# Columns of several groups as 64 columns twice in a tile, any set of groups, first fit in two passes

## The chip, the core and the metric

The kernel runs on one core of a Trainium2 chip. The metric is the device time of one execution in microseconds, the median of three timed runs: 1469.44 us (1468.46 to 1476.89). The profile is of one further execution of the same program.

## The reference

For x of shape (8, 4096, 256), a sparse non-negative adj of (4096, 4096) and a weight W of (256, 256), all float32:

```
A_norm = relu((adj + adj.T) * 0.5)
d      = rowsum(A_norm) ** -0.5           # 0 where the sum is 0
L_norm = I - d[:, None] * A_norm * d[None, :]
out    = layernorm(x + relu(L_norm @ (x @ W)))   # L_norm is shared by the 8 batches
```

Entry (n, m) of adj is drawn with a probability that falls with n and with m, so low rows and columns are dense and the others sparse. The 8 batches of 256 features are treated as 2048 columns, so that the sum is a 4096 x 4096 sparse matrix times a 4096 x 2048 dense one.

## The kernel before, in words

**First stage** (to about 587 us of the profiled execution). Blocks of adj are loaded on SP's queue, transposed on PE (L516), added to their mirror image on DVE (L520), halved and cut at zero on ACT (L524), and stored to `a_dram`. DVE sums each row over groups of 32 columns (L527), and POOL turns the sums into flags, `uses` (L528). The row factors r come from the same sums. g = r * (x W) is formed on PE (L616, L627) and stored to `g_dram`, 4096 rows of 2048 floats (8 KB). Block 0 of the output is multiplied here from whole blocks (L585).

**Second stage.** The other 31 blocks of 128 output rows are worked in 16 units `u` of two blocks (the last has one), in the order `SEQ`. a_dram is symmetric, so the columns that a block needs are rows of a_dram: for a unit, a column m counts only if one of its 8 groups of 32 output rows uses it (4 groups in each block b). The used columns are gathered into tiles of 128: an a-row (32, 128 or 256 floats) and a g-row (2048 floats) for each. The first 2 x 128 columns are used by everybody; they are two resident hub tiles (`g_hub`, a-rows `gh` loaded at L1020).

A tile has two halves of 64 slots, and each half belongs to one kind, a mask of the groups for which its columns are multiplied. There are 15 kinds, `KINDS`: one group alone, pairs of groups, the whole of one block, and 0 for anything (the rest). `CAPS[u][k]` says how many halves the kind k has in unit u and `FIRST[u][k]` where they begin. A tile whose halves have one group each is called alone. In the tables of this case there are 256 tiles, 152 of them alone.

*Lists.* Which column goes into which slot is found on the chip, some units ahead. `patterns` makes the mask of each column on DVE and compares it with the kinds; `count` multiplies by a triangle of ones on PE (L300, L301) to rank the columns of a kind; `place` fits them to the kinds' room, those left over to others, and `count_rest`/`place_rest` the rest; `spread` (L429) and `collect` (L450) turn the slots into lists by products with one-hot tiles, and `index` writes the row numbers `gi` and `ai`. The constants that these steps use are set by memsets on POOL (L218, L219, L225). A dense pass behind the second stage runs only if a list has no room.

*Gathers.* For each tile POOL issues two indirect transfers, the a-rows (L1032) and the g-rows (L1047), into a ring of 12 tiles. A gather is issued once a slot of the ring is free; `gather_ahead` ties it to a product on PE so that the gathers keep pace with the steps.

*Steps.* `steps_of` writes the order of the products. A product takes a piece of PE's array: rows x columns, where 128 rows means all slots of a tile, 64 rows one half of it, and the columns are those of 1, 2 or 4 groups. A step runs over the four chunks c of 512 g-columns, and in each over the products that together fill the array: one of 128x128, two of 128x64, four of 128x32, two of 64x128 or eight of 64x32. The planner picks one such shape for each step. There are 234 steps; 62 belong to the hub tiles. All products of a block add into four banks of PSUM, one for each chunk.

*Blocks end.* When a block's last product is done, ACT evicts its four banks (L788) and DVE adds x and normalises. A unit's block 0 ends four steps ahead of its block 1; in these four steps the lists' products borrow its banks.

The loop over steps is at the end of the function, `product` at L1257 issues one product (L1263).

## Time and profile before

| what | value |
|---|---|
| timed runs, median (lowest, highest) | 1469.44 us (1468.46, 1476.89) |
| profiled execution, its span | 1496.2 us |
| granted TensorE clock, mean | 0.981 |
| first stage, second stage, behind the last product | 0 to 587, to 1484, to 1496 us |
| busy: PE, DVE, POOL, ACT | 1420.1, 1025.2, 745.6, 368.7 us |
| products of the second stage (L1263), busy | 644.8 us (gathered tiles), 226.6 us (hubs) |
| gathers on POOL, a-rows and g-rows | 256 and 256 |
| moved in all; in queue 0, which the gathers use | 540.52 MB; 281.94 MB |

The profiled execution took 26.8 us longer than the median of the timed runs. In the rows that follow, L12 is line 12 of the kernel, PE is TensorE's matmuls and PEld its weight loads. "64*32" is the piece of the array (rows times columns), "64x512" what is moved through it. A float32 product of 512 columns has two matmul records. A matmul's end is modelled and overlaps its successor, so that 600 ns of one isn't the distance between two: that is read from the starts. What stands behind "idle before" is the time for which the engine stood still ahead of the group, and what ended it; "issue" is a wait that the profile doesn't explain.

### The profile page before, as it was taken

Reading aid. Unit: us, or ns where it says so; the run is one execution under the profiler, and the core shown is the slowest. Engines: PE = TensorE matmul, PEld = TensorE weight load, DVE = VectorE, ACT = ScalarE, POOL = GpSimd, SP = SyncE. Lnnn points to the kernel's source line nnn. Section 1 sums busy time; section 2 is a strip of 40 time slices with the busy share of each in tenths; the row PEclk is TensorE's granted clock in tenths of the full one; section 3 lists DMA queues with packets and bytes.
Section 4 is the critical chain, followed back from the end, with each engine's and each line's share of the span. In section 5 each row is a group of like instructions: output and inputs, shape, how many; then the busy total and the mean of one; then the engine's idle time right before and its main releaser. Section 6 shows DMA issues by size and latency. Waiting matters only on the chain.

```text
span 1496.2 us, 20479 instructions
## 1 busy us (share of the span) xinstructions
PE 1420.1 (95%) x6768; PEld 757.9 (51%) x6768; DVE 1025.2 (69%) x3010; ACT 368.7 (25%) x462; POOL 745.6 (50%) x1547
## 2 busy tenths in 40 slices
PE   7998988979999999999999999999999999998996
PEld 6777877766777764333333334333333333333342
DVE  4767558889596752356569678789898079797454
ACT  4555545434544460010100100100110011001102
POOL 2444010010322336756577677577677646666762
PEclk9999999989999999999999999999999999999998
DMA  9999999999999999979899899999999979988995
GB/s 340 360 377 381 406 346 337 393 385 338 379 356 341 371 392 373 373 270 379 332 377 379 338 402 407 366 388 403 398 382 377 387 259 341 354 316 321 402 404 220
DMA packets 215265, 540.52 MB, mean 361 GB/s; under 512 B 17751, under 2 KB 107527, under 8 KB 180839
## 3 DMA queue, kind: packets, MB, share of 16 engines
q0 software_dynamic: 53808, 281.94, 48.5%
q1 hardware_dynamic: 93200, 126.62, 24.4%
q10 hardware_dynamic: 68144, 130.58, 23.0%
q8 instruction: 56, 0.92, 0.2%
q14 instruction: 57, 0.46, 0.1%
HBM read 425.72 MB, written 136.34 MB: 376 GB/s over the span
## 4 chain that ended last, share of the span: by engine, by line
PE 62%; DMA 14%; DVE 11%; issue 7%; POOL 3%; ACT 3%; ACTq 0%; another core or an unknown queue 0%; DVEq 0%; POOLq 0%; SPq 0%
PE py L1263 45%; PE pg L627 8%; DMA a_dram<-sym 6%; DVE sym L520 4%; DMA g<-g_dram,gi 3%; PE xtr L616 3%; PE lead L585 3%; PE tr L516 3%; DMA xin<-in_x_dram 2%; POOL ga L1032 2%; ACT sym L524 1%; DVE sums L527 1%; POOL g L1047 1%; DMA g_dram<-held 1%; PE lists L450 1%
## 5 line engine op out<-in xcount | busy, mean ns | idle before, releaser
L1263 PE MATMUL py<-g,ga 128*32 128x512 f32 (+4 forms) x2880 | 644.8, 606 | 12.3 <-DMA g<-g_dram,gi 7.2
L1263 PEld LDWEIGHTS py<-g,ga 128*32 128x32 f32 (+4 forms) x2880 | 226.0, 138 | 402.0 <-issue 374.4
L1032 POOL DMA_INDIRECT ga<-a_dram,ai x256 | 277.6, 1084 | 181.3 <-issue 62.2
L1047 POOL DMA_INDIRECT g<-g_dram,gi x256 | 284.5, 1111 | 92.9 <-issue 77.6
L788 ACT ACTIVATE y<-py,minus_r 128x512 f32<-128x512 f32 x120 | 80.2, 686 | 796.3 <-PE py L1263 545.9
L627 PE MATMUL pg<-w_sb,xt 128*128 128x256 f32 x1024 | 233.4, 387 | 6.5 <-ACT xt L617 5.7
L1263 PE MATMUL py<-g_hub,gh 128*128 128x512 f32 x496 | 226.6, 601 | 0.5 <-DVE low L465 0.3
L627 PEld LDWEIGHTS pg<-w_sb,xt 128*128 128x128 f32 x1024 | 196.9, 195 | 34.5 <-ACT xt L617 6.6
L520 DVE TENSOR_TENSOR sym<-tr,adj 128x512 f32<-128x512 f32 x256 | 162.3, 684 | 59.0 <-PE tr L516 54.1
L527 DVE TENSOR_REDUCE sums<-sym 128x64 f32<-128x2048 f32 x64 | 145.7, 2282 | 69.5 <-ACT sym L524 69.5
L528 POOL TENSOR_SCALAR uses<-sums 128x64 uint8<-128x64 f32 x64 | 26.7, 417 | 271.1 <-DVE sums L527 236.9
L516 PE MATMUL tr<-ident,adj 128*128 128x128 f32 x1024 | 137.1, 281 | 20.5 <-DVE sym L520 14.3
L1263 PEld LDWEIGHTS py<-g_hub,gh 128*128 128x128 f32 x496 | 90.5, 190 | 123.6 <-issue 116.8
L524 ACT ACTIVATE sym<-sym 128x2048 f32<-128x2048 f32 x64 | 122.7, 1917 | 122.8 <-DVE sym L520 118.6
L516 PEld LDWEIGHTS tr<-ident,adj 128*128 128x128 f32 x1024 | 115.8, 143 | 50.9 <-DVE sym L520 31.1
L242 DVE TENSOR_TENSOR_SCAN incl_r<-carry,lists 128x32 f32<-128x32 bf16 x13 | 2.9, 221 | 182.0 <-PE lists L397 176.0
L429 DVE TENSOR_TENSOR hot<-iota_q,at 128x1024 bf16<-128x1024 f32 x64 | 74.5, 1220 | 34.0 <-PE lead L585 32.1
L798 DVE TENSOR_TENSOR xr<-xr,y 128x2048 f32<-128x2048 f32 x31 | 70.8, 2284 | 38.8 <-ACT y L788 32.1
L616 PE MATMUL xtr<-ident,xin 128*128 128x128 f32 x512 | 74.5, 299 | 17.9 <-DVE sym L520 9.0
L831 DVE TENSOR_SCALAR xr<-xr,mv,root 128x256 f32<-128x256 f32 x248 | 85.1, 416 | 1.1
L807 DVE BATCH_NORM_STATS2 stats<-xr 128x6 f32<-128x256 f32 x248 | 84.0, 413 | 1.1
L585 PE MATMUL lead<-gt,strip 128*128 128x512 f32 x176 | 82.4, 593 | 0.0
(164 smaller groups left out, 1040.1 us busy)
## 6 DMA issues: line engine op xcount, KB each, us to landing
adj<-in_adj_dram SPq DMA_DIRECT2D x64, 1024.0 KB
a_dram<-sym ACTq DMA_DIRECT2D x64, 1024.0 KB
out_dram<-xr SPq DMA_DIRECT2D x31, 1024.0 KB
xr<-in_x_dram ACTq DMA_DIRECT2D x28, 1024.0 KB
xin<-in_x_dram SPq DMA_DIRECT2D x44, 512.0 KB
g_dram<-gt ACTq DMA_DIRECT2D x22, 1024.0 KB
xin<-in_x_dram POOLq DMA_DIRECT2D x20, 512.0 KB
g_dram<-held ACTq DMA_DIRECT2D x10, 1024.0 KB
```

Source lines behind the costliest of these rows:

```text
L516: ins = nc.tensor.transpose(pt[:, c * P : (c + 1) * P], tji[:, c, a * P : (a + 1) * P], ident)
L520: nc.vector.tensor_add(sym[:, a, :], pt, tij[:, a, :])
L524: nc.scalar.activation(sym, sym, AF.Relu, scale=0.5)
L527: nc.vector.tensor_reduce(sums, sym.rearrange("p a (c q) -> p a c q", q=E), AX.X, ALU.add)
L585: nc.tensor.matmul(lead[c], lhsT=strip, rhs=g[:, c * S : (c + 1) * S], start=not done, stop=len(done) == NB - 1, skip_group_check=True,)
L616: nc.tensor.transpose(pt[:, k, c, :], xin[b // H][:, b % H + k, c * P : (c + 1) * P], ident)
L627: ins = nc.tensor.matmul(pg[:, k * FO : (k + 1) * FO], lhsT=xt[:, b + k, c, :], rhs=w_sb[:, c, :], start=(c == 0), stop=(c == FC - 1),)
L807: nc.vector.bn_stats(stats[:, b, :], z[:, b, :])
L831: nc.vector.tensor_scalar(z[:, b, :], z[:, b, :], mv[:, b, 0:1], rstd[:, b : b + 1], ALU.subtract, ALU.mult,)
L1032: rows = nc.gpsimd.indirect_dma_start(out=at if both else at[:, : E if one else P], out_offset=None, in_=a_pairs if both else a_groups if ...
L1047: nc.gpsimd.indirect_dma_start(out=gt, out_offset=None, in_=g_dram, in_offset=bass.IndirectOffsetOnAxis(ap=gi[:, t : t + 1], axis=0), boun ...
L1263: return nc.tensor.matmul(py[2 * u + 1 + b][c][cols, :], lhsT=at[ps, off + cols.start : off + cols.stop], rhs=gt[ps, c * S : (c + 1) * S], ...
```

## The change

**Tiles.** A table `UNITS` replaces `KINDS`, `CAPS` and `FIRST`. For each unit it gives the number of alone tiles of each of the 8 groups, a list of kinds (mask, halves, place), the halves of the rest, the order in which the planner meets the tiles, and its two settings, how many tiles it looks at (`reach`) and how far block 1 stands back (`lag`). A mask may be any set of groups. A column goes to the first kind that covers its groups, in two passes: alone tiles and the first 7 kinds, then all kinds; what has no place then is the rest.

An alone tile is as before: 128 columns, one group, 128x32 products. Every other tile is a pair of halves, and a half is now 64 columns that stand twice in the tile: partitions 0 to 63 hold the first 1024 floats of their g-rows and partitions 64 to 127 the other 1024. So a half fills 128 partitions x 1024 floats, and the two halves of a tile lie side by side. A group's product with a half is four products of 64x32, in two rows of the array at once: the upper one writes chunks 0 and 1, the lower one chunks 2 and 3. There are 253 tiles, 133 of them alone, and 120 pairs with 232 halves.

**Gathers.** A pair tile has one gather of a-rows (into one of 8 buffers `gw`, mostly 256 floats wide) and one of g half rows for each half. Of POOL's issues in the second stage:

Before, a run of tiles at the start of the stage; `ga` are a-rows, `g` g-rows, the numbers only tell buffers apart:

```order
L1032 DMA ga_5775<-a_dram,ai_4117 128x32
L1047 DMA g_5739<-g_dram,gi_4115 128x2048
L1032 DMA ga_5776<-a_dram,ai_4117 128x128
L1047 DMA g_5743<-g_dram,gi_4115 128x2048
L1032 DMA ga_5777<-a_dram,ai_4117 128x256
L1047 DMA g_5747<-g_dram,gi_4115 128x2048
```

and after, at the same place:

```order
L1084 DMA ga_5071<-a_dram,ai_3431 128x32
L1102 DMA g_5032<-g_dram,gi_3428 128x2048
L1084 DMA gw_5081<-a_dram,ai_3431 128x256
L1102 DMA g_5036<-g_dram,gi_3428 128x1024 x2
L1084 DMA gw_5082<-a_dram,ai_3431 128x256
L1102 DMA g_5040<-g_dram,gi_3428 128x1024 x2
```

An alone tile keeps its two gathers; a pair tile has three. In the whole stage 512 gathers became 618 (253 of a-rows, 133 of whole g-rows, 232 of half rows). The columns gathered are 29 952 before and after.

**Swaps.** Each half's a-rows are needed in both rows of the array. ACT copies them to the other 64 partitions, into one of 6 buffers `gs`, up to three steps ahead of the tile's first use (`swap_ahead`). On ACT's queue, at the start of the second stage, behind the evictions of block 0 (L912):

```order
L912 ACTIVATE y_5177<-lead_168,minus_r 128x512
L1135 COPY gs_5089<-gw_5081 64x256 x2
L1135 COPY gs_5090<-gw_5082 64x256 x2
L1135 COPY gs_5091<-gw_5083 64x256 x2
L1135 COPY gs_5092<-gw_5084 64x256 x2
```

There are 232 such copies, where ACT's queue had none.

**Steps.** `steps_of` now fills, for each of the 4 columns of 32, the four chunks of a step: with one 128x32 product of an alone tile (four chunks), or with two (half, group) products (two chunks each, in both rows). It takes whatever comes first in its order, so that a step may hold both shapes. On PE, unit 1, the first step of gathered tiles, behind a hub's last product; before:

```order
L1263 MATMUL py_0_3_5872<-g_hub_5719,gh_0_5784 128x512
L1263 MATMUL py_0_0_5869<-g_5727,ga_5772 32x512
L1263 MATMUL py_0_0_5869<-g_5731,ga_5773 32x512
L1263 MATMUL py_0_0_5869<-g_5735,ga_5774 32x512
L1263 MATMUL py_0_0_5869<-g_5739,ga_5775 32x512
L1263 MATMUL py_0_1_5870<-g_5727,ga_5772 32x512
```

and after (products with `gw` or `gs` are of 64x32, those with `ga` of 128x32; `py_0_2` is block 0, chunk 2):

```order
L1365 MATMUL py_0_0_5193<-g_5024,ga_5069 32x512
L1365 MATMUL py_0_0_5193<-g_5028,ga_5070 32x512
L1365 MATMUL py_0_0_5193<-g_5032,ga_5071 32x512
L1365 MATMUL py_0_0_5193<-g_5036,gw_5081 32x512
L1365 MATMUL py_0_2_5195<-g_5036,gs_5089 32x512
L1365 MATMUL py_0_1_5194<-g_5024,ga_5069 32x512
L1365 MATMUL py_0_1_5194<-g_5028,ga_5070 32x512
L1365 MATMUL py_0_1_5194<-g_5032,ga_5071 32x512
L1365 MATMUL py_0_1_5194<-g_5036,gw_5081 32x512
L1365 MATMUL py_0_3_5196<-g_5036,gs_5089 32x512
```

Four alone tiles filled a step; now three do with a half beside them. There are 204 steps: 62 of hubs, 142 others, of which 78 hold both shapes. The first block's end still lies four steps ahead of the unit's end.

**Lists and constants.** The constants come from one table loaded on ACT's queue in place of 752 memsets on POOL. `match` finds the first fitting kind with bit operations on DVE; `count`, `count_more` and `count_rest` rank on PE. A one-hot tile of `collect` is 64 wide instead of 128, and each of its products is issued twice, for the two halves of PE's columns.

The core of the diff:

```
-            with queue("pool"):
-                nc.gpsimd.indirect_dma_start(
-                    out=gt,
-                    out_offset=None,
-                    in_=g_dram,
-                    in_offset=bass.IndirectOffsetOnAxis(ap=gi[:, t : t + 1], axis=0),
...
+            for h in range(1 if who == ALONE else len(pair(u, t))):
+                k = t if who == ALONE else 2 * t + h
+                end = N if who == ALONE else 2 * N + 1
+                with queue("pool"):
+                    nc.gpsimd.indirect_dma_start(
+                        out=gt if who == ALONE else gt[:, h * HG : (h + 1) * HG],
+                        out_offset=None,
+                        in_=g_dram if who == ALONE else g_halves,
+                        in_offset=bass.IndirectOffsetOnAxis(ap=gi[:, k : k + 1], axis=0),
...
+        def swap_ahead(q):
...
+            while swaps and first_use[swaps[0]] <= q + SOON and free(swap_of, swapped % SWAP):
...
+                for h in range(len(pair(u, t))):
+                    to, of = slice((1 - h) * L, (2 - h) * L), slice(h * L, (h + 1) * L)
+                    with queue("act"):
+                        nc.scalar.copy(sw[to, :width], at[of, :width])
...
+                u, t = order[asked]
+                if t >= alone[u] and not free(wide_of, widened % WIDE):
+                    break
                 gather(asked, behind)
```

```
+        while any(todo.values()):
+            near = [t for t in todo if todo[t]][:reach]
+            ops = sorted((op for t in near for op in todo[t]), key=lambda op: turn[op[0]] + lag * op[2])
+            step = []
+            for j in range(QU):
+                at = 0
+                while at < NC:
+                    op = next((op for op in ops if op[3] == j and (op[1] is not None or at == 0)), None)
+                    if op is None:
+                        break
+                    ops.remove(op)
+                    todo[op[0]].remove(op)
+                    step.append((op, at))
+                    at += NC if op[1] is None else NC // 2
+            out.append(step)
...
+                for r in range(2):
+                    ps = slice(r * L, (r + 1) * L)
+                    of = at if r == h else sw
+                    rhs = gt[ps, h * HG + sub * S : h * HG + (sub + 1) * S]
+                    parts.append((2 * r + sub, of[ps, own_rows], rhs))
...
-            for c in range(NC):
-                for op in step:
-                    rows = slice(0, P) if op[1] is None else slice(op[1] * L, (op[1] + 1) * L)
-                    cols = slice(op[3] * E, (op[3] + op[4]) * E)
-                    ins = product(u, op, c, rows, cols, first, op in last)
...
+            for sub in range(NC):
+                for op, at in step:
+                    if at <= sub < at + (NC if op[1] is None else NC // 2):
+                        ins = product(u, op, sub - at, opens[op], last[op])
```

```
     def collect(u, pl):
...
+            for h in range(2):
+                nc.tensor.matmul(
+                    pl[h * L : (h + 1) * L],
+                    lhsT=hot[:, m],
...
+    table = nc.inline_tensor(np.concatenate(parts)[None], name="table").ap()
+    tables = const.tile([P, ends[-1]], I32, name="tables")
+    nc.scalar.dma_start(tables, table.to_broadcast([P, ends[-1]]))
```

919 lines of the change are left out of this document (510 added, 409 removed), and 32 rows, old and new, of tables (CAPS, FIRST).

## The prediction

> **What bounds the kernel now.** The page first, for the balance over the span (busy time and share of each engine, then tenths in 40 slices):
>
> ```profile
> PE 1420.1 (95%) x6768; PEld 757.9 (51%) x6768; DVE 1025.2 (69%) x3010; ACT 368.7 (25%) x462; POOL 745.6 (50%) x1547
> PE   7998988979999999999999999999999999998996
> DMA  9999999999999999979899899999999979988995
> ```
>
> TensorE and the DMA engines are both busy throughout. The windows tell which one is waited for in the second stage (length; busy time of PE, PEld, DVE, ACT, POOL; granted clock; DMA share; GB/s), and the group of its products shows their idle time:
>
> ```profile
> 587.00:1480.00 893.00, 874.26 (x3843) 333.06 (x3841) 617.88 (x2216) 81.06 (x122) 586.70 (x561) 0.99 0.95 362
> 1000.00:1100.00 100.00, 98.25 (x443) 37.88 (x436) 84.04 (x306) 10.88 (x16) 69.92 (x67) 1.00 1.02 401
> L1263 PE MATMUL py<-g,ga 128*32 128x512 f32 (+4 forms) x2880 | 644.8, 606 | 12.3 <-DMA g<-g_dram,gi 7.2
> ```
>
> PE is busy for 874 of 893 us and its products waited 12.3 us in all. So PE's own sequence sets the end; the transfers keep up with little to spare. What the products cost is read from two timelines, of PE and of its weight loads (start, duration, shape of the array's piece, number of records, idle time before):
>
> ```profile
> 587.10 3.60 PE L1263 MATMUL py<-g_hub,gh 128*128 128x512 f32 x8
> 590.63 3.64 PE L1263 MATMUL py<-g,ga 128*32 128x512 f32 x32
> 594.20 3.27 PE L1263 MATMUL py<-g_hub,gh 128*128 128x512 f32 x7
> ...
> 640.47 0.18 PEld L1263 LDWEIGHTS py<-g,ga 64*32 64x32 f32 x16 [0.76 <-DMA g<-g_dram,gi]
> ...
> 645.41 0.20 PEld L1263 LDWEIGHTS py<-g,ga 64*32 64x32 f32 x6 [0.59 <-issue]
> 646.44 0.16 PEld L1263 LDWEIGHTS py<-g,ga 128*32 128x32 f32 x8 [0.84 <-issue]
> 646.90 0.13 PEld L1263 LDWEIGHTS py<-g,ga 128*32 128x32 f32 x4 [0.30 <-issue]
> 647.33 0.13 PEld L1263 LDWEIGHTS py<-g,ga 128*32 128x32 f32 x4 [0.30 <-issue]
> ```
>
> A 512-column product has two records. Steady loads come 0.43 us apart (646.90 to 647.33), so one pass of the filled array over 512 columns takes 0.86 us (0.858 by finer rows), whether it is one 128x128, four 128x32 or eight 64x32. A step is four passes, 3.43 us; from start to start it is 3.53 to 3.57 where the shape changes. So a change costs about 0.09 us when the array is full on both sides. The row at 646.44 matters most: the first load of the new shape stands 0.84 us idle, where within a shape 0.30 is usual. The next shape's weights aren't loaded while the old one streams. Every change of the second stage looks like this; no row shows products of two shapes at once, because the old order has one shape in a step.
>
> **The change, part by part.** *Products.* The old order has 234 steps, 936 passes and 156 changes: 936 x 0.858 + 156 x 0.093 = 817.6 us. With stalls in the 64x32 steps (27.9, below), list products and waits this fills the 893 us. The new order has 204 steps, of which 62 are hubs and 78 mix 128x32 with 64x32 inside each chunk. Two readings bound it.
>
> If the two shapes share the array, each column of 32 goes at its own pace and only changes to and from 128x128 count: 792 passes and 31 changes, 682.4 us, 135 less than before.
>
> If a change waits for the old shape to end, as at 646.44, the mixed chunk falls apart. In the order shown above, three 128x32 products fill three quarters of a pass; then two 64x32 products take a pass for a quarter of the array; then three 128x32 again. This step makes 8 passes and 8 changes, 7.6 us instead of 3.43. Going through the whole order so gives 1180 passes and 717 changes: 1180 x 0.858 + 717 x 0.093 = 1079.1 us, 261.5 more than before.
>
> I take the second. Of the rows there are, 646.44 is the nearest: the same two shapes in succession. It is not proof, since all pieces of the array were occupied there; but the weights could have been loaded ahead of it, as they are within a shape, and weren't.
>
> The Trainium skill, TensorEngine Tiling (Array Packing), section Key Properties, says "Mode switching requires drain: Changing tiling mode (not just tile) drains the TensorE", and its list of configurations keeps 128x32 and 64x32 apart. The trace agrees as far as it goes (0.84 us of idle loads at each change); by this rule the sum is the second one, and without it the first.
>
> *Lists.* The products that collect the lists double from 512 to 1024, each for 64 columns instead of 128.
>
> ```profile
> 723.04 0.32 PEld L450 LDWEIGHTS <-hot 128*128 128x128 bf16 x10 [0.62 <-issue]
> L225 POOL MEMSET group_of<- 64x1 bf16 x304 | 29.1, 96 | 10.9
> L524 ACT ACTIVATE sym<-sym 128x2048 f32<-128x2048 f32 x64 | 122.7, 1917 | 122.8 <-DVE sym L520 118.6 <-DMA g_dram<-gt 4.2
> L788 ACT ACTIVATE y<-py,minus_r 128x512 f32<-128x512 f32 x120 | 80.2, 686 | 796.3 <-PE py L1263 545.9 <-remote 117.8 <-DVE root L826 34.7
> L617 ACT COPY xt<-xtr 128x512 f32<-128x512 f32 x128 | 67.9, 593 | 52.7 <-PE xtr L616 51.7 <-ACT held L652 0.4
> ```
>
> At 0.032 us each (10 in 0.32) 512 more cost 16 us, or nothing if two halves run side by side; I take 10.
>
> *Constants.* 752 memsets leave POOL's program for one table (the largest group, 29.1 us, is shown). They lay in the first stage, where POOL is a quarter busy: nothing gained.
>
> *Swaps.* ACT gets 232 copies of 64x256 or 64x128. The nearest row, a 128x512 copy, takes 593 ns; an upper bound is 232 x 0.593 = 138 us, a lower one half of it. ACT is busy 81 of 893 us in this stage, and a swap is asked for three steps ahead, over 10 us: nothing, hidden by ACT's idle time. Evictions of L788 queue behind a swap whose a-rows are late, and the next unit's products wait for those evictions. At most one step (3.5 us) at one tile in ten, some 40 us; below nothing I see no way.
>
> *Gathers.* Each of the 120 pair tiles brings its g in two half rows: 618 gathers for 512, over nearly the same bytes.
>
> ```profile
> 568.10 1.06 POOL L1032 DMA_INDIRECT ga<-a_dram,ai  x1 [0.82 <-DMA a_dram<-diag]
> ...
> 911.83 0.95 POOL L1032 DMA_INDIRECT ga<-a_dram,ai  x1 [0.30 <-issue]
> 913.09 1.01 POOL L1047 DMA_INDIRECT g<-g_dram,gi  x1 [0.30 <-DMA g<-g_dram,gi]
> 914.41 0.94 POOL L1032 DMA_INDIRECT ga<-a_dram,ai  x1 [0.30 <-issue]
> ...
> 1461.58 1.00 POOL L1047 DMA_INDIRECT g<-g_dram,gi  x1 [0.99 <-DMA g<-g_dram,gi]
> ...
> L1047 POOL DMA_INDIRECT g<-g_dram,gi x256 | 284.5, 1111 | 92.9 <-issue 77.6 <-DMA g<-g_dram,gi 10.1 <-DMA gh<-a_dram 2.3
> L1032 POOL DMA_INDIRECT ga<-a_dram,ai x256 | 277.6, 1084 | 181.3 <-issue 62.2 <-PE py L1263 51.3 <-PE lists L300 20.0
> L1020 POOL DMA_DIRECT2D gh<-a_dram x62 | 36.2, 584 | 25.1 <-PE py L1263 10.6 <-DMA g<-g_dram,gi 6.0 <-issue 3.2
> ```
>
> From start to start an a-gather takes 1.26 us and a g-gather 1.32 (rows at 911.83 to 914.41); with the groups' means (1084 and 1111 ns) and the same 0.30 between, 1.39 and 1.42. A half-row gather has as many rows, so I price it like a whole one; half of that is its lower bound. With 62 hub loads at 0.9: 253 x 1.26 + 365 x 1.32 + 56 = 856 us, at most 253 x 1.39 + 365 x 1.42 + 56 = 926. While PE takes 1079 us this is hidden. If PE takes only 682, it is the bound.
>
> **The sum.** 1496.2 + 261.5 + 10 = 1767.7 us for a profiled execution. The span stands 26.8 us above the median of the timed runs, 1469.4; taking the difference over, **1741 us**. Its own range: without lists, 1725, and some overlap at the ends of runs, down to 1690; with 40 us of swap waits, 1780; so 1690 to 1800.
>
> **The rivals.** *Shapes share the array, POOL sets the pace.* For it: pieces in different columns touch nothing in common, and no row of before shows them refusing. Against it: 646.44. Then the last gather starts at 568 + 856 to 926 = 1424 to 1494 instead of 1461.6; the 34.6 us behind it stay, less the 26.8: 1432 to 1502, middle about 1465, no change.
>
> *Shapes share it and the gathers keep up: faster.* One mechanism, at POOL: a half-row gather costs well under a whole one. It decides from a POOL sum below about 845 us (568 + 845 + 34.6 - 26.8 = 1421). At half the price, 232 gathers save 153 us, POOL needs 703 and the transfers bind: 893 us x 362 GB/s = 323 MB, at the best window's 401 GB/s 806 us. From 587, with 13 us behind the last product, less 26.8: about 1380. Between the two, 1420.
>
> *The stalls of the 64x32 steps are real.* The seven 64x32 steps of before take longer than their 3.55 us. The first (640.47 to 646.44) takes 5.97; the last is
>
> ```profile
> 1342.26 0.15 PEld L1263 LDWEIGHTS py<-g,ga 64*32 64x32 f32 x8 [0.76 <-DMA g<-g_dram,gi]
> ...
> 1354.12 0.30 PEld L1263 LDWEIGHTS py<-g,ga 128*128 128x128 f32 x2 [0.89 <-issue]
> L1263 PE MATMUL py<-g,ga 64*32 64x512 f32 x384 | 44.9, 660 | 8.3 <-issue 4.0 <-DMA g<-g_dram,gi 3.6
> L1263 PE MATMUL py<-g,ga 64*128 64x512 f32 x112 | 25.9, 602 | 0.0
> ```
>
> 11.86 us. Together the seven take 52.7, where 7 x 3.55 is 24.9: 27.9 too much, with nothing named as the cause. This is nearly what the span has over the median (26.8), so I hold it for something of the profiled execution alone. If the timed runs have it too, 384 records cost 27.9 us, and the 6416 of the change up to 466 more: 1900 and above.
>
> The Trainium skill (the same page, section Restrictions and Gotchas) says that different row tiles cannot access one PSUM bank at the same time. Before, both halves of a chunk write one bank; now they write two. By this rule the stalls would go with the change, and the time stay with the other cases; but the 64x128 products write one bank from two halves as well, and stand at 602 ns without a stall.
>
> **How the numbers follow.** Shapes wait for each other: 0.50 (1741). Shared and POOL-bound: 0.25 (1465). Shared and faster: 0.18 (1420). Stalls or swap waits beyond that: 0.07 (1900). The likeliest is 1741. Since the shared cases hold 0.43, the range takes in most of them: 1425 to 1800; left out are the stalls and the fastest part of the shared cases, together near 0.15. About 1% (1455 to 1484) is what a measurement can tell from no change. Faster: all but a little of 0.18, and a quarter of the POOL case, 0.24. Same: nearly half of the POOL case and a little more, 0.13. Slower: the rest, 0.63.
>
> **What would show it.** Right: in a mixed step the weight loads of 64x32 start 0.7 us or more after those of 128x32, each chunk takes about 1.9 us, POOL waits for PE more than now, and DMA falls to about 280 GB/s in the second stage (323 MB over some 1155 us). Wrong: mixed steps of 3.4 to 3.6 us, PE idle before L1365 by gathers, POOL busy for over 75 us in each 100 (0.95 of 1.26 us, since the 0.30 between gathers isn't counted). If the stalls belong to the profiled execution, its span will stand further above the timed median than now.

## The result, and the profile after

The changed kernel takes 1979.99 us (median of four runs, 1974.80 to 1987.03) against 1469.54 us for the kernel before: a ratio of 1.3465 [1.3422, 1.3508], 510 us slower. The forecast was 1741 us, with a range to 1800: the direction is right, the size is 239 us short. The profiled execution has a span of 1980.0 us and is one of the four timed runs.

The page of the changed kernel, to be held against the three lines of the page before (busy times; granted clock and DMA share in 40 slices):

```profile
PE 1768.7 (89%) x11912; PEld 717.0 (36%) x11912; DVE 1047.9 (53%) x2771; ACT 456.4 (23%) x694; POOL 810.7 (41%) x887
PEclk9999998999999999899899998879997898999998
DMA  9999998899998684477894856487892483898296
```

The DMA engines, 0.95 busy in the second stage before, now have holes. The clock dips in the same part of the span. The second stage as one window (columns as in the prediction's windows), and the groups of its products:

```profile
598.40:1966.80 1368.40, 1223.92 (x8943) 296.70 (x8943) 613.86 (x2006) 171.42 (x357) 695.06 (x668) 0.94 0.69 242
```

```profile
L1365 PE MATMUL py<-g,gw 64*32 64x512 f32 x3208 | 596.4, 618 | 28.7 <-DMA g<-g_dram,gi 28.7
L1365 PE MATMUL py<-g,gs 64*32 64x512 f32 x3208 | 596.2, 618 | 9.1 <-DMA g<-g_dram,gi 8.9
L1365 PE MATMUL py<-g,ga 128*32 128x512 f32 x1064 | 420.3, 637 | 92.8 <-DMA g<-g_dram,gi 92.7
```

The stage is 1368 us long where it was 896 (587.1 to 1483.2). PE is busy for 1224 of them, 347 more than before, and idle for 145, where it was idle for 19. So there are two losses: PE has more to do, and it waits for g. The waits of PE over the whole execution (us, times, longest):

```profile
PE py L1365 <- DMA g<-g_dram,gi: 130.3, 44, 7.3
...
PE q L416 <- DVE ahead_of L369: 13.2, 1, 13.2
PE py L1365 <- DVE low L582: 11.5, 6, 3.1
```

130 us of waiting for gathers stand where the kernel before had 7.2.

**More to do.** The weight loads of a mixed step, two chunks of it:

```profile
1305.09 0.14 PEld L1365 LDWEIGHTS py<-g,ga 128*32 128x32 f32 x4 [0.84 <-issue]
1306.07 0.10 PEld L1365 LDWEIGHTS py<-g,gs 64*32 64x32 f32 x1 [0.84 <-issue]
...
1307.07 0.14 PEld L1365 LDWEIGHTS py<-g,ga 128*32 128x32 f32 x2 [0.84 <-issue]
1308.04 0.10 PEld L1365 LDWEIGHTS py<-g,gw 64*32 64x32 f32 x1 [0.84 <-issue]
```

The shapes take turns. The idle time of 0.84 us that stood at one step in several before now stands twice in every chunk, and a chunk takes 1.98 us (1305.09 to 1307.07) where a filled pass takes 0.86. This is the forecast's second reading, row for row.

**Waiting, and its second price.** One step with a late tile, on PE:

```profile
1282.35 1.04 PE L1365 MATMUL py<-g,ga 128*32 128x512 f32 x2
1284.20 0.61 PE L1365 MATMUL py<-g,gw 64*32 64x512 f32 x1 [0.80 <-DMA g<-g_dram,gi]
...
1289.81 1.03 PE L1365 MATMUL py<-g,gw 64*32 64x512 f32 x1 [4.56 <-DMA g<-g_dram,gi]
...
1298.52 1.92 PE L1365 MATMUL py<-g,ga 128*32 128x512 f32 x4 [6.79 <-DMA g<-g_dram,gi]
1300.36 1.06 PE L1365 MATMUL py<-g,gw 64*32 64x512 f32 x1
...
1304.08 0.64 PE L1365 MATMUL py<-g,gs 64*32 64x512 f32 x1
```

PE waits 4.56 us and then 6.79 us. Behind each wait the records take 1.03 to 1.06 us instead of 0.61, until about 1304. As windows (the last three columns are granted clock, DMA share and GB/s):

```profile
1298.50:1304.00 5.50, 5.49 (x16) 0.59 (x16) 0.00 (x0) 1.21 (x3) 4.28 (x5) 0.50 0.90 318
1304.00:1310.00 6.00, 6.00 (x64) 1.41 (x70) 0.00 (x0) 0.81 (x2) 3.55 (x5) 0.99 1.04 386
```

PE runs at half its clock (0.50) for some microseconds after it has stood still. The Trainium skill (TensorE: Matmul & The Clock Gate, Part 1) says that the array falls to half its clock after at least one idle window of about 3.4 us, and comes back after at least one busy window of that length; these rows agree, with 5.6 us of half speed behind the second wait. So a wait of this length is paid twice. A short one isn't: behind the 0.80 us at 1284.20 the record still takes 0.61 us.

POOL isn't short of time when this happens. Its timeline ahead of the late step, and its groups:

```profile
1265.24 0.96 POOL L1084 DMA_INDIRECT gw<-a_dram,ai  x1 [19.87 <-issue]
1266.51 0.99 POOL L1102 DMA_INDIRECT g<-g_dram,gi  x1 [0.30 <-DVE slot L523]
1267.80 1.04 POOL L1102 DMA_INDIRECT g<-g_dram,gi  x1 [0.30 <-issue]
```

```profile
L1102 POOL DMA_INDIRECT g<-g_dram,gi x365 | 394.4, 1081 | 118.8 <-issue 106.0 <-DMA g<-g_dram,gi 7.7 <-DMA gh<-a_dram 1.4
L1084 POOL DMA_INDIRECT ga<-a_dram,ai x133 | 141.0, 1060 | 295.6 <-PE py L1365 242.3 <-issue 24.8 <-PE lists L508 23.2
L1084 POOL DMA_INDIRECT gw<-a_dram,ai x120 | 133.8, 1115 | 251.4 <-issue 205.2 <-ACT y L912 24.1 <-PE py L1365 15.3
```

POOL stood idle for 19.87 us, then issued gathers back to back, and this burst came too late. Over the stage it waits 258 us for PE (242.3 and 15.3; 51.3 before). The planner looks at up to nine tiles at once, so many of the ring's 12 tiles are half used and none is free; then several come free together, and the pacing asks for only one or two of them in a step. Counted through the order in the code, the unit that ends here has all 12 places taken and ten of them half used four steps before its end, and all 12 free one step before it.

**The sum.** I added up, over the second stage, the distance from each product's start to the next one's, and put each to what stood between the two (records of over 0.9 us count as half clock; a distance at a wait holds the record ahead of it as well, about 0.43 us):

| us | before | after |
|---|---|---|
| products, shape unchanged | 750.4 | 701.8 |
| a change of shape between (before 130, after 625 times) | 68.1 | 326.5 |
| at half clock, shape unchanged; changed | 7.0; 1.0 | 69.8; 40.9 |
| waits for g | 10.2 | 160.1 |
| lists' products between | 34.6 | 49.3 |
| waits for DVE (lists) | 9.7 | 20.0 |
| waits without a name | 15.2 | 0 |
| second stage | 896 | 1368 |

About half of what the half-clock rows hold would be there at full clock too. So the products, with their changes, went from 822 to some 1084 us (1139 less 55); late gathers cost 150 in waits, and the clock some 50, which I put to them as well; lists and list waits cost 25, the stage begins 11 us later, and the 15 us of waits without a name are gone. Together this is the 484 us between the two profiled spans.

### The profile page after: what moved, and what is told of

The parts are those of the page before. It is cut to its first block, busy times and chain, and to the rows that moved or that the text cites. A ratio compares the mean times of both kernels' runs of the same rounds, so it can differ in the third digit from the quotient of the medians.

```text
span 1980.0 us, 30359 instructions
## 1 busy us (share of the span) xinstructions
PE 1768.7 (89%) x11912; PEld 717.0 (36%) x11912; DVE 1047.9 (53%) x2771; ACT 456.4 (23%) x694; POOL 810.7 (41%) x887
## 3 DMA queue, kind: packets, MB, share of 16 engines
q0 software_dynamic: 69840, 287.63, 40.9%
## 5 line engine op out<-in xcount | busy, mean ns | idle before, releaser
L1365 PE MATMUL py<-g,gw 64*32 64x512 f32 x3208 | 596.4, 618 | 28.7 <-DMA g<-g_dram,gi 28.7
L1365 PE MATMUL py<-g,gs 64*32 64x512 f32 x3208 | 596.2, 618 | 9.1 <-DMA g<-g_dram,gi 8.9
L1365 PE MATMUL py<-g,ga 128*32 128x512 f32 x1064 | 420.3, 637 | 92.8 <-DMA g<-g_dram,gi 92.7
L1102 POOL DMA_INDIRECT g<-g_dram,gi x365 | 394.4, 1081 | 118.8 <-issue 106.0
L1084 POOL DMA_INDIRECT ga<-a_dram,ai x133 | 141.0, 1060 | 295.6 <-PE py L1365 242.3
L1135 ACT COPY gs<-gw 64x256 f32<-64x256 f32 (+1 forms) x232 | 90.5, 391 | 648.0 <-DMA gw<-a_dram,ai 637.5
L1084 POOL DMA_INDIRECT gw<-a_dram,ai x120 | 133.8, 1115 | 251.4 <-issue 205.2
L1365 PE MATMUL py<-g_hub,gh 128*128 128x512 f32 x496 | 224.5, 610 | 11.5 <-DVE low L582 11.5
L1365 PEld LDWEIGHTS py<-g,ga 128*32 128x32 f32 x1064 | 56.8, 110 | 421.9 <-issue 402.1
L1365 PEld LDWEIGHTS py<-g,gw 64*32 64x32 f32 x3208 | 116.7, 108 | 251.8 <-issue 238.3
L912 ACT ACTIVATE y<-py,minus_r 128x512 f32<-128x512 f32 x120 | 78.7, 687 | 527.7 <-PE py L1365 515.3
L1365 PEld LDWEIGHTS py<-g,gs 64*32 64x32 f32 x3208 | 116.7, 108 | 224.7 <-issue 219.0
```

Of the source, the lines that this page charges most:

```text
L912: nc.scalar.activation(y.rearrange("p b o -> p (b o)")[:, c * S : (c + 1) * S], py[c], AF.Relu, scale=minus_r[:, i : i + 1],)
L1084: rows = nc.gpsimd.indirect_dma_start(out=at[:, :width], out_offset=None, in_={2: a_pairs, ALONE: a_groups}.get(who, a_rows), in_offset=ba ...
L1102: nc.gpsimd.indirect_dma_start(out=gt if who == ALONE else gt[:, h * HG : (h + 1) * HG], out_offset=None, in_=g_dram if who == ALONE else ...
L1135: nc.scalar.copy(sw[to, :width], at[of, :width])
L1365: ins = nc.tensor.matmul(banks[c][cols, :], lhsT=rows, rhs=rhs, start=first, stop=last, skip_group_check=True,)
```

## The experiments

The kernel before took 1469 to 1471 us on some of the chips used and 1488 to 1497 us on others. Every ratio is with its runs on the same chip. Each chip was used in one sitting only, so that whether the chip or the sitting makes the difference isn't known; "chip" stands for both here. The changed kernel itself ran only where the kernel before takes 1469 us, while e1 to e8 ran on chips of the slower kind: a time of theirs set against 1979.99 us holds the chip's difference as well, which was not measured for the changed kernel.

**First group: the shapes, or the gathers?** *e1: no change of shape.* Each half product as two 128x32 ones instead of four 64x32: the same array area, one shape. A product then sums over both partition halves, which is not the reference's sum.

```
-                for r in range(2):
-                    ps = slice(r * L, (r + 1) * L)
-                    of = at if r == h else sw
-                    rhs = gt[ps, h * HG + sub * S : h * HG + (sub + 1) * S]
-                    parts.append((2 * r + sub, of[ps, own_rows], rhs))
+                of = at if sub == 0 else sw
+                rhs = gt[:, h * HG + sub * S : h * HG + (sub + 1) * S]
+                parts.append((2 * h + sub, of[:, own_rows], rhs))
```

> Each (half, group) is multiplied by two 128x32 products in its column of the array instead of four 64x32, so that all gathered products have one shape; gathers, swaps, lists, steps and their order stay. (The two halves of a tile are mixed up in this: that part of the product is changed.) Theory, a change of shape lets the old shape run out: 792 passes and about 90 changes, 690 us of PE instead of about 1100; the gathers then set the pace, 1430 to 1600 us. Rival, the late gathers alone make the change slow: they are the same, so 1900 to 2000 us. Rival, 64x32 products are slow by themselves: also below 1600, told apart by the kernel with steps of one shape.

Measured: 1783.83 us, ratio 1.1946 [1.1864, 1.2027]. PE's waits of this kernel:

```profile
PE py L1363 <- DMA g<-g_dram,gi: 223.0, 83, 8.1
```

The changes' distances fell from 367 us to 8.9, and the time by some 196 us (on a chip where the kernel before is 23 us slower), so the drain is real. The time lies above the theory's 1430 to 1600 us and below the rival's 1900: with the products faster, the waits for g rose from 130 to 223 us and the mean clock fell to 0.913. The drains had been covering part of the gathers' lateness: there are two losses, and neither is the whole.

*e2: the shapes sorted within a step.* First all 128x32 products of a step, then all 64x32: 141 changes for 667.

```
+            for part in (True, False):
...
-                    if at <= sub < at + (NC if op[1] is None else NC // 2):
+                        if (op[1] is None) == part and at <= sub < at + (NC if op[1] is None else NC // 2):
```

> Within each step all 128x32 products come first, over the four chunks, then all 64x32; nothing else moves. Changes fall from 717 to 182, passes from 1180 to 1098: 1098 x 0.858 + 182 x 0.12 = 964 us of PE for 1098. Theory, changes let the array run out: 135 us less, about 1845 us. Rival, late gathers: within 20 us of 1980. Rival, 64x32 products slow by themselves: within 20 us of 1980.

Measured: 1918.27 us, ratio 1.2846 [1.2758, 1.2934]. This is 62 us less than the changed kernel, where 135 were expected. The distances at changes hold 74 us instead of 367 (each has a pass's 0.43 us in it), but the products in between rose from 702 to 903: each shape's share of a step still fills only part of the columns, and an empty column takes the same 0.86 us. The dear thing about a mixed step is less the change than the broken passes.

*e3: one shape in a step.* The planner fills a step with one shape, from five tiles at most; 227 steps.

```
-            near = [t for t in todo if todo[t]][:reach]
+            near = [t for t in todo if todo[t]][: min(reach, 5)]
...
+            for single in (True, False):
+                left, step = [op for op in ops if (op[1] is None) == single], []
...
+            out.append(best[1])
```

> The planner gives each step one shape, four 128x32 or up to eight 64x32 in each chunk, and looks at 5 tiles at most; tiles, gathers and swaps stay. 227 steps, 886 passes, 110 changes: 773 us of PE for 1098. Theory, changes let the array run out: 325 us less, and what then is left of the waits (250 us with the slow clock behind them) is open: 1480 to 1680 us. Rival, 64x32 products slow by themselves: there are as many as before, 1900 us or more. Rival, late gathers: 1900 us or more.

Measured: 1746.49 us, ratio 1.1669 [1.1592, 1.1746], above what was expected. The products cost what they should (754 us, and 44 at changes, where before has 750 and 69), and still 58 us of waits for g, 99 us at half clock and 87 us of waits without a name remain.

*e4: gathers as soon as there is room.* The pacing of the gathers is dropped.

```
-            for _ in range(room if behind is None else min(room, 1 + (room > SLACK))):
+            for _ in range(room):
```

> Gathers are issued for every free place of the ring at each step, instead of one, or two when over five places are free. Order of the products as in the change. Theory, shapes 258 us and late gathers with the slow clock behind them 250 us of the loss: if the pace of one or two tiles a step makes them late, 1750 to 1900 us; if the ring itself is full, within 20 us of 1980. Rival, late gathers alone: below 1700 us.

Measured: 2024.19 us, ratio 1.3555 [1.3461, 1.365]. None of the expected ranges holds this time. PE's idle time for g fell from 130 to 20 us with the reach of nine left as it was, so the pacing has its share in the lateness. But waits without a name rose to 113 us, and PE stood idle 11 us for evictions and 21 for a source that the profile calls "remote". On this chip issuing earlier is no cure; what it does on a chip without the unnamed waits was not run.

*e6: five tiles in view.* Only the planner's reach changes; 652 shape changes stay.

```
-            near = [t for t in todo if todo[t]][:reach]
+            near = [t for t in todo if todo[t]][: min(reach, 5)]
```

> The change, with shapes mixed as in it, but its planner looks at 5 tiles at most instead of 5 to 9. Passes 1155 for 1180, changes 652 for 717: 29 us less of PE. A tile is now asked for two steps or more ahead of its first product (30 tiles of the change only one or two), so the ring holds fewer tiles half used. Theory B, tiles held in the ring: the waits for gathers (160 us) and the slow clock behind them (about 55 us lost) fall by over half, 1820 to 1870 us. Theory A, the third gather: as many gathers as before, so 1940 us or more.

Measured: 1869.63 us, ratio 1.2564 [1.2514, 1.2615]. PE's waits for g and the second stage as a window:

```profile
PE py L1365 <- DMA g<-g_dram,gi: 9.0, 2, 5.3
```

```profile
597.80:1855.90 1258.10, 1189.21 (x8945) 323.67 (x8943) 611.63 (x2006) 170.61 (x357) 692.98 (x668) 0.97 0.77 263
```

130 us of waits became 9, with the same gathers and the same POOL time. So POOL's total isn't what made them late. With e4 this says that a tile is late when it is asked for too few steps ahead, which the reach and the pacing settle together: counted through the code, 30 of the 253 tiles are asked for only one or two steps before their first product in the change, 4 with five tiles in view (e6), 8 without the pacing (e4). The granted clock rose from 0.94 to 0.97. The stage shrank by 110 us, less than the 200 that waits and clock had cost: PE now idles 22 us for the lists' `low` (11.5 in the change), and this chip adds waits without a name, some 40 us.

**Second group: both taken out, then the third gather.** *e9: e1's products and e6's reach together.*

```
-            near = [t for t in todo if todo[t]][:reach]
+            near = [t for t in todo if todo[t]][: min(reach, 5)]
...
+                parts.append((2 * h + sub, of[:, own_rows], rhs))
```

> The change with both suspects taken out at once: every product of a half is issued as two 128x32 ones (so that no shape changes inside a step; the halves of a product are mixed, and its sums are not the reference's), and the planner looks at five tiles at most. Theory A, the losses are separate and add up (shape changes; gathers that come late because up to nine tiles stand half used in the ring): from the 1784 us of the one-shape kernel go its 278 us of waits for g and half of its 150 us of slow clock, some 12 steps of 3.5 us come back and some 30 to 50 us of unnamed stalls at the denser gathers: 1480 to 1590 us, waits for g below 60 us. Theory B, with the products this cheap POOL's 618 gathers are the bound whatever the order: waits for g stay above 120 us and the time at 1600 us or more.

Measured: 1609.08 us, ratio 1.0929 [1.0886, 1.0972].

*e10: the same with one half-row gather for each pair tile*, 506 gathers in all; the second half's g is left out, and with it 55 MB.

```
-            for h in range(1 if who == ALONE else len(pair(u, t))):
+            for h in range(1):
...
-                rhs = gt[:, h * HG + sub * S : h * HG + (sub + 1) * S]
+                rhs = gt[:, sub * S : (sub + 1) * S]
```

> The kernel of the run before with one half-row gather for each pair tile instead of two (the second half's g is left out, its products use the first one's): 506 gathers for 618. Theory A (gathers cost only through lateness, which the five tiles took away): within 30 us of the run before. Theory B (the third gather of a pair tile costs by itself, as in the kernel before with its g in two gathers, 96 us): 60 to 130 us less, about 1420 to 1500, so that the change without its drains and its extra gathers would stand near the kernel before or below it. If both, drains and gathers, are the whole loss, it is faster than before by up to 5 per cent; if it stays above 1500, something else in the change costs as well.

Measured: 1517.77 us, ratio 1.0326 [1.0287, 1.0365]. Waits and second stage, first of the kernel with 618 gathers:

```profile
PE py L1363 <- DMA g<-g_dram,gi: 101.1, 51, 8.9
PE py L1363 <- DVE low L582: 46.9, 12, 8.7
```

```profile
598.50:1591.60 993.10, 841.71 (x5736) 289.20 (x5735) 611.31 (x2005) 173.26 (x357) 695.50 (x667) 0.93 0.93 332
```

and of the one with 506:

```profile
PE py L1363 <- DMA g<-g_dram,gi: 47.2, 21, 8.8
PE py L1363 <- DVE low L582: 45.2, 10, 8.3
```

```profile
598.60:1496.80 898.20, 803.24 (x5736) 283.59 (x5735) 610.16 (x2005) 173.11 (x357) 584.46 (x555) 0.95 0.88 305
```

e9 fits its theory B: 1609 us, and waits for g of 132 us counted as distances, as the expectation counts them (101 of idle time). With cheap products PE is idle for 151 of 993 us, while POOL is taken for 896 of them (695.5 and 667 times the 0.30 between) and the DMA engines for 0.93. Taking 112 gathers and their bytes away saves 91 us, as e10's theory B says, so now the gathers bound the time; whether by POOL or by the bytes, this pair doesn't part. The time stays above that theory's 1420 to 1500 us. What is left, 3.3%, is late lists (45 us of waits for `low`), late gathers (47 us) and the later start. The packing as such does save: products of one shape take 678 us of distances here, 750 before. But this gain isn't the change's to have, since 64x32 beside 128x32 doesn't run in this way.

**Third group: what a third gather costs.** *e5: the kernel before with 104 tiles' g in two gathers of half rows*; the same bytes, 616 gathers.

```
+            for h in range(1 if one else 2):
+                w = G if one else G // 2
...
+                        out=gt[:, h * w : (h + 1) * w],
...
+                        element_offset=h * w,
```

> The kernel before, with the g-rows of each of its 104 tiles of several groups brought by two gathers of 1024 floats instead of one of 2048; nothing else. POOL then needs 256 x 1.26 + 360 x 1.32 + 56 = 853 us of the 893 of the second stage, for 716. Theory A, the third gather of a pair tile makes POOL late: 1 to 5% slower than before. Theory B, the gathers of the change are late because its steps hold many tiles of the ring half used: within 1% of before.

Measured: 1584.48 us, ratio 1.063 [1.0569, 1.0691]; 96 us, more than either theory allowed. The 360 gathers of g, whole and half rows together, take 1116 ns of POOL on average, where 256 whole ones took 1111: a half-row gather costs as much as a whole one, as the forecast priced it. With the bytes equal, the number of gathers and of rows is dear.

*e11: split by slots instead*, 64 whole rows in each gather (the second 64 slots get the first 64's rows, so the output differs).

```
+            for h in range(1 if one else 2):
+                ps = slice(0, P) if one else slice(h * L, (h + 1) * L)
...
+                        in_offset=bass.IndirectOffsetOnAxis(ap=gi[: P if one else L, t : t + 1], axis=0),
```

> The kernel before; the g of the 104 tiles that are not alone comes in two gathers, but split by slots: 64 whole rows of 8 KB each, instead of two half rows for each of 128 slots as in the run that cost 96 us (the second 64 slots get the first 64's rows again, so the products with them are not the reference's). The number of gathers is 616 as there, the packets and bytes stay those of the kernel before. Theory A, the price of the extra gathers lies with POOL and its queue, by the instruction: 50 to 110 us more than before, PE's unnamed stalls well above the 15 us of before. Theory B, it lies with the rows that are described and moved (78848 rows in that run, 65536 in the kernel before and here): within 20 us of before.

Measured: 1729.61 us, ratio 1.1566 [1.1514, 1.1618]. Both theories missed. The second stage shows why:

```profile
584.00:1709.90 1125.90, 978.17 (x3875) 354.49 (x3873) 617.62 (x2217) 82.59 (x125) 687.55 (x664) 0.93 1.00 296
```

The DMA engines are busy all the time (1.00) and move only 296 GB/s, where the kernel before moved 361 at 0.95. Gathers of this form move more slowly (64 partitions at a time, or the same rows twice: that wasn't parted), so this run tells nothing of POOL.

*e12: POOL busy, no gathers added.* Four memsets behind the g-gather of 104 tiles.

```
+            if not one:
+                with queue("pool"):
+                    for _ in range(4):
+                        nc.gpsimd.memset(busy, 0.0)
```

> The kernel before, with four memsets of 256 floats on POOL behind the g-gather of each of the 104 tiles that are not alone: about 1.2 us of POOL's time for each (204 ns for 128 floats in the profile of before), 125 us in all, as much as the 104 extra gathers of 1.12 us take it, but nothing for the DMA engines. Theory C, POOL's time is what binds (756 of its 896 us in the second stage are gathers, hub loads and the 0.30 us between): 60 to 120 us more than before. Theory D, the price lies behind POOL, in what the gathers bring into the queue: within 20 us of before.

Measured: 1561.37 us, ratio 1.0438 [1.0401, 1.0475]: 66 us for 133 us of POOL's time (416 memsets of 321 ns), without one byte more. So POOL's time alone has a price, about two thirds of what the split gathers cost. Some 18 us of it are waits without a name (33, for 15 before).

*e8: the third gather left out of the kernel of e3* (half of the pair tiles' g left out with it).

```
-            for h in range(1 if who == ALONE else len(pair(u, t))):
+            for h in range(1):
...
-                    rhs = gt[ps, h * HG + sub * S : h * HG + (sub + 1) * S]
+                    rhs = gt[ps, sub * S : (sub + 1) * S]
```

> The kernel with one shape a step, but of each pair tile only the first half's g-rows are gathered, and both halves' products read them. (Half of the pair tiles' g is left out of the computation.) POOL needs 253 x 1.26 + 253 x 1.32 + 56 = 709 us, as little as before, and some 57 MB less are moved. If late gathers and the clock behind them are what is left: 1600 to 1660 us. If PE's stalls without a named cause and the waits for lists are: 1690 us or more.

Measured: 1644.50 us, ratio 1.1051 [1.1001, 1.1102], from 1.1669 (e3, on another chip of the slower kind): 92 us or so, as expected if late gathers are what is left, and the same size as in the pair of e9 and e10.

*e7: the kernel of e3 with the hub steps spread* and the pacing tighter.

```
-    SLACK = 5
+    SLACK = 2
...
+        out.insert(min(6, last), late[0])
```

> The kernel with one shape a step, but of a unit's three hub steps at the start one is moved behind the sixth step and one ahead of block 1's first product, and two tiles are asked for in a step as soon as over two places are free (five in the change). 227 steps, 886 passes. If late gathers and the slow clock behind them are what is left over the kernel before: 1640 to 1720 us, for 1746. If PE's stalls without a named cause and the waits for lists are: 1725 us or more.

Measured: 1776.96 us, ratio 1.1944 [1.1905, 1.1983]; slower than e3. Waits for g halved (58 to 29 us), waits without a name rose from 87 to 138. Moving the gathers in time moves the loss.

*e13 and e14: the 62 hub loads on SP's queue*, in the kernel before and in that of e3; 55 us less for POOL.

```
-            with queue("pool"):
-                nc.gpsimd.dma_start(
+            with queue("sp"):
+                nc.sync.dma_start(
```

> The kernel before with the 62 loads of the hub tiles' a-rows on SP's queue instead of POOL's: 62 x (0.58 + 0.30) = 55 us less of POOL's time in the second stage, the same transfers. Theory C, POOL's time binds beside PE already in the kernel before (the memsets cost 66 us for 133 us of POOL): 15 to 40 us faster. Theory D', POOL binds only once more is put on it, and the kernel before has room: within 10 us of before. Slower, if the loads come late behind SP's stores: then PE's waits name gh.

> The change with one shape in a step and five tiles (the run of 1746 us), and the hub loads on SP's queue: 55 us less of POOL's time. Theory C: 25 to 60 us below that run's ratio of 1.167, so about 1.13 to 1.15, with fewer waits for g and fewer unnamed stalls of PE (57 and 87 us there). Theory D', what is left of the loss is PE's own (stalls, lists, changes): within 1 per cent of 1.167.

Measured: 1466.65 us, ratio 0.9968 [0.9951, 0.9985], and 1642.80 us, ratio 1.1171 [1.1137, 1.1205]. The kernel before gains 0.3%: POOL has room there. The second looks like theory C, and lies below its 1.13, but it ran on a chip where the kernel before takes 1469 us, and e3 on one where it takes 1493. That had to be told apart.

**Fourth group: the same four kernels on one chip.** Kernels of e5, e12, e3 and e14, unchanged.

> The kernel before with the g of 104 tiles in two gathers of half rows (96 us slower where the kernel before takes 1488 us). In the profiles so far PE's unnamed stalls of 0.7 us stand in all runs on chips where the kernel before takes 1488 to 1495 us (15 us in the kernel before itself, 82 in this one), and in none where it takes 1469 to 1471. Theory S, two thirds of the price were these stalls, and they are the chip's: on a chip of the 1470 kind at most 40 us more than before, stalls below 5 us. Theory P, the price is POOL's time and the stalls only show it: 70 us or more here too, then as waits for g or lists. On a chip of the 1490 kind both expect the 96 us again.

> The kernel before with four memsets behind the g-gathers of 104 tiles (66 us slower on a chip of the 1490 kind). Theory S: at most 40 us on a chip of the 1470 kind (33 us of unnamed stalls less 15 were in it). Theory P: 50 us or more.

> The change with one shape in a step and five tiles (ratio 1.167 on a chip of the 1490 kind, 87 us of unnamed stalls). Theory S: on a chip of the 1470 kind a ratio of 1.10 to 1.13, the same as with the hub loads on SP's queue. Theory P: 1.15 or more, with waits for g above 100 us.

> The same with the hub loads on SP's queue, on the same chip as the run before. Theory S: within 1 per cent of it, so that the 1.117 of the earlier run was the chip's doing. Theory P: 25 to 60 us faster than it.

Measured, beside 1497.03 us for the kernel before: 1603.44 (1.0726 [1.0676, 1.0776]), 1564.57 (1.0471 [1.0419, 1.0522]), 1755.76 (1.1738 [1.168, 1.1796]) and 1744.27 us (1.167 [1.1611, 1.1728]). The chip was again of the slower kind, so the first two only repeat. The last two answer: beside each other the hub loads' place is worth 0.7% and not 5%. The 101 us between 1642.80 and 1744.27, for one and the same program, are the chip's. The 64x32 products of that program, on the first chip:

```profile
L1378 PE MATMUL py<-g,gw 64*32 64x512 f32 x3208 | 413.0, 610 | 14.0 <-DMA g<-g_dram,gi 14.0
```

and on the second, with a stretch of PE's timeline there:

```profile
L1378 PE MATMUL py<-g,gw 64*32 64x512 f32 x3208 | 514.0, 611 | 18.3 <-issue 9.5 <-DMA g<-g_dram,gi 7.2
```

```profile
609.82 0.61 PE L1378 MATMUL py<-g,gw 64*32 64x512 f32 x1 [0.44 <-issue]
610.55 1.32 PE L1378 MATMUL py<-g,gs 64*32 64x512 f32 x3
612.70 0.59 PE L1378 MATMUL py<-g,gs 64*32 64x512 f32 x1 [0.83 <-issue]
```

The same 3208 records occupy 413 us on one and 514 on the other. On the second, products trickle in one or two at a time, 0.7 to 1.4 us apart (the three of the row at 610.55 start at 610.55, 611.25 and 611.27), where eight should come every 0.43 us, and the trace names nothing that they wait for. The loading of instructions doesn't show as the cause: queue 8, of the kind "instruction", has 97 transfers of about 0.98 us (median) in either run, and none of them lies in the 8 us ahead of this stretch. Such stalls stand in all 14 runs on chips of the slower kind (29 to 138 us in waits without a name) and in none of the five profiles taken where the kernel before takes 1469 to 1471 us (at most one wait, 1.7 us), the changed kernel's own among them. In some pairs they grow with the gathers: 15 us in the kernel before, 82 with its gathers split, 87 in e3, 38 with e3's third gather left out. But the number of gathers alone doesn't set them: e1, e2 and e6 have the same 618 as e3 and only some 30 to 45 us, and e12, with the 512 of the kernel before, has 33 us.

## Why the prediction was right in kind and wrong in size

*Products: right.* "1180 x 0.858 + 717 x 0.093 = 1079.1 us", from 817.6: some 1084 were measured, from 822. A change in the table takes 0.522 us from start to start on average where a repeat takes 0.43, so its price was 0.093 too; e1, which has no changes, shows that the drain is the cause. The drain rule that stood beside this sum (the Trainium skill, TensorEngine Tiling (Array Packing), Key Properties) agrees with the 0.84 us of idle loads at each change above. The two rivals with shared shapes are out: no mixed step ran near 3.5 us.

*Gathers: the step that failed.* "While PE takes 1079 us this is hidden" priced the gathers at nothing. Their sum was right: POOL's second stage is 695 us of work and 668 times 0.30 between, 895 us, inside the forecast's 856 to 926. But a sum that is smaller than PE's says nothing of when each tile comes. The step compared two totals and never asked how many tiles of the ring are free when a burst is needed. The runs put in its place: 150 us of waits, by the planner's reach over nine tiles and the pacing (idle time 130 us, 9 in e6, 20 in e4), and some 50 us by the clock that halves after them, which the forecast had no term for. 200 of the 239 us missing are this term. The rest is the lists and the later start (36 us where 10 were priced) and the 26.8 us taken off for the profile, of which 15 came.

The trace of before showed it in small. The prediction says of the seven 64x32 steps that nothing is named as the cause of their 27.9 us too much, and counts the last one (1342.26 to 1354.12) with 8.3 of them. On PE that step reads

```profile
1344.08 1.05 PE L1263 MATMUL py<-g,ga 64*32 64x512 f32 x4 [0.76 <-DMA g<-g_dram,gi]
1347.93 6.89 PE L1263 MATMUL py<-g,ga 64*32 64x512 f32 x53 [2.80 <-DMA g<-g_dram,gi]
```

and the loads behind the second wait come 0.85 us apart (1348.76, 1349.61, 1350.46) instead of 0.43: a late gather, and half the clock behind it (granted 0.50 from 1347.9 to 1353), here after 0.76 and 2.80 us of idle time.

*The range.* "Without lists, 1725" takes 16 us off where the sum had put in 10; 1731 follows from it.

*Lists.* Priced at 10 us on PE; it is 15 there (34.6 to 49.3). What wasn't priced is the chain on DVE: PE waits 13.2 us in the first stage for `ahead_of` (L369), the scan in the new ranking, and the second stage begins 11 us later; waits for lists add 10 more.

*Constants*: no gain shows, as said. *Swaps* cost PE nothing, as said: no wait of it names `gs`. POOL's gathers into `gw` wait 24.1 us for ACT, which was not followed up.

*The stalls of the 64x32 steps.* "I hold it for something of the profiled execution alone": taking 26.8 us off was near right, since the 15 us of unnamed waits are gone, but the reason was not: that is luck. The timed spans of the changed kernel and its profiled span agree within 0.7%, so no profile stretches anything. The stalls are in timed runs too, on some chips. On such a chip the kernel before takes 1488 to 1497 us, about its profiled span, so that the profile of before very likely came from one: inferred, since its profile was not repeated on the other kind. The closest to it, e13 on a chip of the faster kind, has the first unit's 64x32 step at its full rate:

```profile
635.04 0.15 PEld L1263 LDWEIGHTS py<-g,ga 64*32 64x32 f32 x8 [0.28 <-issue]
635.47 0.15 PEld L1263 LDWEIGHTS py<-g,ga 64*32 64x32 f32 x8 [0.28 <-issue]
635.90 0.15 PEld L1263 LDWEIGHTS py<-g,ga 64*32 64x32 f32 x8 [0.28 <-issue]
```

Eight loads come every 0.43 us: the same step took 5.97 us in the profile of before. The prediction's sentence that "both halves of a chunk write one bank" before the change is wrong. By the order that `steps_of` makes, in all seven 64x32 steps and all seven 64x128 steps of the kernel before the upper half's products belong to block 0 and the lower half's to block 1, and the two blocks have different banks. So two rows of the array wrote different banks before as well as after, and the rule that the prediction weighed (the Trainium skill, the same page, Restrictions and Gotchas) is neither borne out nor refuted: no run here has two rows write one bank. It explains no stall of these kernels. The fourth rival's figure, 1900 and above, was met by another mechanism.

*What would show it.* Loads of the second shape 0.7 us or later: 0.98. A chunk of about 1.9 us: 1.98. POOL waiting more for PE: 258 us for 51. DMA at about 280 GB/s: 242, because the stage is 1368 us long and not 1155.

*What stays open.* What the stalls without a name are, why some kernels have more of them, and whether the chip or the sitting brings them. How the price of a third gather divides: on the slower chips 96 to 106 us in the kernel before, of which POOL's time explains some 66 (e12); the split gathers were never run on a chip without stalls, and the 91 us between e9 and e10 there take 55 MB away with the gathers. No kernel tried beats the kernel before by more than e13's 0.3%.

## What to carry to other kernels

Count passes by what really runs together: products of two shapes of the array take turns here, so a mixed step pays for every column that its shape leaves empty, and sorting the shapes within a step mends only a part (62 us in e2). A queue whose total fits under the bound can still be late in each step; look at how much of the ring a step holds open, and price a wait of PE of some microseconds at more than its length, since the clock halved behind waits of 2.80, 4.56 and 6.79 us here. Read what ended each wait of a slow step before its cause is called unnamed. Where the profiled span and the timed runs differ, ask which chip each came from before a stall is set aside.

## What the runs showed of the hardware that was not expected

- One program took 1642.80 us on one chip and 1744.27 on another, by stalls of PE that the trace doesn't name (products 0.7 to 1.4 us apart).
- Gathers of 64 rows of 8 KB into 64 partitions, each list used twice, move slowly: queue 0 took 55.2% of 1725.4 us for 291.92 MB with such gathers, 48.5% of 1496.2 us for 281.94 MB without.
- A gather's time on POOL hardly depends on its size: in the changed kernel half rows of 4 KB take 1075 ns on average, whole rows of 8 KB 1091, alone tiles' a-rows of 128 bytes 1060.
- Behind a wait of 6.79 us PE ran at half speed for 5.6 us (records of 1.06 us, 0.59 at full clock).
